# A four-layer graph kernel: one Strassen product moved to another PSUM bank, and seven products for ten pairs of the third layer's first block

## The chip, the cores and the metric

The kernel runs on one core of one Trainium2 chip. The metric is the device time of one execution in microseconds, as a median of several runs. A profile is taken of one execution apart; its span runs from the first to the last instruction that the profiler saw.

Five engines work side by side[...]: TensorE (PE in the profile, its weight loads PEld), VectorE (DVE), ScalarE (ACT), GpSimd (POOL) and the queue of SyncE (SP), which issues DMAs. [...]

## The reference, cut to what matters

Four graph layers in float32 run over 4096 nodes with 256 features and one adjacency matrix of 4096 x 4096. Each is an attention over the neighbours, followed by a residual sum and a layernorm over the 256 features. The change lies in the third layer, and in helpers that it shares with the fourth:

```python
def _L2_gnn_ref(x, adj, W, a):
    h = x @ W
    e = (h @ a[:D, 0])[:, None] + (h @ a[D:, 0])[None, :]
    e = jnp.where(e > 0, e, NEG_SLOPE * e)
    attention = jax.nn.softmax(jnp.where(adj > 0, e, MASK_VAL), axis=1)
    return jax.nn.elu(attention @ h)

x = _layernorm(x + _L0_gnn_ref(...))   # four heads, additive scores
x = _layernorm(x + _L1_gnn_ref(...))   # four heads, query and key
x = _layernorm(x + _L2_gnn_ref(x, adj, L2_gnn_W, L2_gnn_a))
x = _layernorm(x + _L3_gnn_ref(...))   # cosine scores, half of the features kept
```

## The kernel before, in words

The features of all nodes stay in SBUF as `X`: 32 tiles of 128 nodes x 256 features. The nodes that receive are taken in eight blocks `b` of 512; for each block a sum over all 32 tiles of sending nodes is built in PSUM. In layers three and four the sending tiles are taken two at a time: `g` counts these 16 pairs (`NP`). Layer three applies its matrix W only after the sum.

**Weights.** `weights(b, g)` of the third layer (`additive_one`) makes the unnormalised attention weights of one pair in `prob`, two tiles of 128 x 512. It issues the mask's DMA on SP (four buffers), computes `r` on ScalarE into PSUM (L566), and joins `r`, a factor of the sending node and the mask on VectorE (L567).

**Sums, plain and with seven products.** The sum of a pair is a product of (2 x 128 sending nodes) x (2 x 128 features) with (2 x 128 sending nodes) x (2 x 256 receiving nodes): a 2 x 2 by 2 x 2 block product. Done plainly it takes eight block products, here four matmuls of 512 columns (L581). Strassen's form in Winograd's variant takes seven matmuls of 256 columns (`product`, L446) on mixed operands. `mix_features` (L429 to L432) makes four mixed feature blocks for two pairs at a time: `mixed[q]` serves pairs 2q and 2q+1, and is made once and used in all blocks. `mix_weights` (L436 to L438) makes four mixed weight blocks for each pair of each block: L436 is on VectorE, L437 and L438 are on GpSimd in the third layer and on VectorE in the fourth.

Block 0 of the third layer is summed plainly into two of the four banks `acc`, because the mixed features are only made while it runs: at each odd `g`, on VectorE. Blocks 1 to 7, and the fourth layer, use seven products.

The seven products of all pairs add up in seven halves of the four banks. `first_half` (L451 to L455) and `second_half` (L459, L460) turn these sums into the four quarters `c` of the result. Bank 3 holds product 0 alone, in its first half; its second half is unused.

**The order.** In the third layer the order on PE, VectorE and ScalarE is written out by hand; GpSimd and SP are ordered by the scheduler. A loop over `i` handles unit `i`'s weights and unit `i - 3`'s sums (`LAG = 3`), and spreads other work over the steps: `finish` brings the block before to its end, `follow` prepares the fourth layer's factors, and the generator `before` brings the last block of the second layer to its end inside block 0. That work joins two partial row sums (L867), transposes on PE (L880, L888, L895), divides and adds (L903 to L912), takes statistics (L156), a root (L161 to L171, partly on GpSimd), scales rows (L186), and takes a dot product per row (L504), from which ScalarE and VectorE make the factors that weights 14 and 15 need (L511 to L513). The last sum of a block is issued ahead of the weights of its step, so that the banks are emptied early.

The fourth layer (`cosine_attention`) is ordered by the scheduler until its ending. Its scores are matmuls of 512 columns (L1118), its mixes are all on VectorE.

## Time and profile before

| what | value |
| --- | --- |
| time, median of 3 runs | 2798.02 us (2794.73 to 2802.38) |
| the profiled execution's own time | 2795.6 us |
| its span | 2793.8 us |
| PE busy | 2774.1 us (99%) |
| VectorE busy | 2289.0 us (82%) |
| ScalarE busy | 1700.7 us (61%) |
| GpSimd busy | 1052.5 us (38%) |
| granted TensorE clock | 1.00 throughout |

The first layer's sums end at 723 us, the second layer's at about 1714 us, the third layer runs from there to about 2165 us, and the fourth to 2794 us. A row of the timeline has its start and its duration in us, the engine, the line of the kernel, what is written and read, the shape, how many instructions it merges, and in brackets how long the engine was idle before it and what ended that. A matmul of float32 leaves two records. "Busy" counts a wait inside an instruction as work.

### The profile page before, as it was taken

Reading aid. Unit: us, or ns where it says so; the run is one execution under the profiler, and the core shown is the slowest. Engines: PE = TensorE matmul, PEld = TensorE weight load, DVE = VectorE, ACT = ScalarE, POOL = GpSimd, SP = SyncE. Lnnn points to the kernel's source line nnn. Section 1 sums busy time; section 2 is a strip of 40 time slices with the busy share of each in tenths; the row PEclk is TensorE's granted clock in tenths of the full one; section 3 lists DMA queues with packets and bytes.
Section 4 is the critical chain, followed back from the end, with each engine's and each line's share of the span. In section 5 each row is a group of like instructions: output and inputs, shape, how many; then the busy total and the mean of one; then the engine's idle time right before and its main releaser. Section 6 shows DMA issues by size and latency. Waiting matters only on the chain. (4 is left out here: it accounts for less than half of the span.)

```text
span 2793.8 us, 50176 instructions
## 1 busy us (share of the span) xinstructions
PE 2774.1 (99%) x19445; PEld 1427.4 (51%) x19445; DVE 2289.0 (82%) x3040; ACT 1700.7 (61%) x2650; POOL 1052.5 (38%) x986
## 2 busy tenths in 40 slices
PE   9999999999999999999999999999999999999999
PEld 5333333333453333333333333788888777777776
DVE  8899999999677788887888878888887877767676
ACT  7899999999336666666666666465556422222222
POOL 0000100100029878778788793345455000000000
PEclk9999999999999999999999999999999999999999
DMA  7566676665339899998988988567778545445442
GB/s 206 107 142 137 139 144 130 137 143 114 70 97 191 186 178 196 191 188 182 197 182 189 192 181 187 168 198 207 183 207 232 121 76 82 74 71 82 75 72 44
DMA packets 275065, 411.92 MB, mean 147 GB/s; under 512 B 54809, under 2 KB 155657, under 8 KB 273930
## 3 DMA queue, kind: packets, MB, share of 16 engines
q0 software_dynamic: 104176, 182.74, 41.3%
q1 hardware_dynamic: 164280, 218.88, 26.7%
q10 hardware_dynamic: 6370, 7.10, 0.7%
q8 instruction: 152, 2.49, 0.4%
q14 instruction: 87, 0.71, 0.1%
HBM read 335.94 MB, written 39.40 MB: 134 GB/s over the span
## 5 line engine op out<-in xcount | busy, mean ns | idle before, releaser
L834 DVE TENSOR_TENSOR prob<-p,mask 128x1024 f32<-128x1024 f32 x512 | 620.0, 1222 | 166.9 <-ACT p L824 159.9
L824 ACT ACTIVATE p<-p,shift 128x1024 f32<-128x1024 f32 x512 | 557.0, 1090 | 317.8 <-PE p L822 317.1
L312 PE MATMUL acc<-prob,V 128*32 128x512 f32 x6144 | 664.0, 592 | 1.2 <-DVE prob L302 1.2
L299 ACT ACTIVATE prob<-row,dst 128x512 f32<-128x512 f32 x1020 | 635.9, 716 | 0.4
L302 DVE SCALAR_TENSOR_TENSOR prob<-prob,mask 128x2048 f32<-128x2048 f32 x256 | 580.6, 2288 | 25.8 <-ACT prob L299 24.8
L844 POOL TENSOR_TENSOR den<-den,prob 128x1024 f32<-128x1024 f32 x220 | 559.8, 2544 | 92.6 <-DVE prob L834 87.2
L822 PE MATMUL p<-qT,kT 64*64 64x512 f32 x4096 | 531.1, 590 | 2.0 <-DVE prob L834 2.0
L858 PE MATMUL acc<-prob,V 64*64 64x512 f32 x4096 | 529.9, 589 | 0.0
L312 PEld LDWEIGHTS acc<-prob,V 128*32 128x32 f32 x6144 | 197.3, 110 | 453.0 <-issue 432.2
L446 PE MATMUL acc<-mix,mixed 128*128 128x256 f32 x1428 | 388.0, 380 | 2.7 <-DVE quarters L460 1.2
L858 PEld LDWEIGHTS acc<-prob,V 64*64 64x64 f32 x4096 | 157.4, 133 | 282.1 <-issue 280.3
L822 PEld LDWEIGHTS p<-qT,kT 64*64 64x64 f32 x4096 | 154.3, 133 | 278.9 <-issue 256.5
L446 PEld LDWEIGHTS acc<-mix,mixed 128*128 128x128 f32 x1428 | 269.5, 190 | 45.0 <-PE acc L446 3.5
L90 POOL COPY tick<-prob 128x1 f32<-128x1 f32 x35 | 38.0, 1086 | 643.0 <-DVE prob L302 642.1
L1130 DVE TENSOR_TENSOR prob<-prob,mask 128x1024 f32<-128x1024 f32 x128 | 156.2, 1220 | 140.5 <-ACT prob L1122 140.1
L850 POOL DMA_DIRECT2D den<-prob x240 | 232.0, 967 | 61.0 <-DVE prob L834 22.3
L446 PE MATMUL acc<-prob,X 128*128 128x256 f32 x952 | 245.7, 380 | 3.4 <-DVE quarters L452 3.3
L1050 POOL DMA_DIRECT2D mask<-in_adjT x64 | 47.7, 745 | 530.1 <-DVE prob L1130 437.6
L446 PEld LDWEIGHTS acc<-prob,X 128*128 128x128 f32 x952 | 180.1, 190 | 84.1 <-issue 56.7
L567 DVE SCALAR_TENSOR_TENSOR prob<-r,own,mask 128x512 f32<-128x512 f32 x252 | 177.1, 744 | 51.3 <-POOL s L169 13.7
L1122 ACT ACTIVATE prob<-p 128x512 f32<-128x512 f32 x144 | 86.1, 598 | 204.1 <-PE p L1118 202.6
L1122 ACT ACTIVATE prob<-g 128x512 f32<-128x512 f32 x112 | 67.0, 598 | 208.7 <-PE g L1118 208.7
(233 smaller groups left out, 2823.1 us busy)
## 6 DMA issues: line engine op xcount, KB each, us to landing
mask<-in_adjT SPq DMA_DIRECT2D x254, 512.0 KB
den<-prob POOLq DMA_DIRECT2D x240, 512.0 KB, 5.3
mask<-edges SPq DMA_DIRECT2D x512, 64.0 KB
mask<-in_adjT POOLq DMA_DIRECT2D x64, 512.0 KB, 5.7
edges<-in_adj POOLq DMA_DIRECT2D x32, 512.0 KB, 9.6
far<-squares SPq DMA_DIRECT2D x16, 512.0 KB
den<-prob SPq DMA_DIRECT2D x16, 512.0 KB
row<-far SPq DMA_DIRECT2D x7, 1024.0 KB
```

The source lines that it names most:

```text
L299: nc.scalar.activation(z[:, h, :], r, AF.Relu, bias=-1.0, scale=dst[:, j, h:h + 1])
L302: nc.vector.scalar_tensor_tensor(z, z, 1.0, mask[m][:, j % MJ, :].unsqueeze(1).to_broadcast([P, H, QW]), OP.add, OP.mult)
L312: nc.tensor.matmul(acc[b][h * G:(h + 1) * G, n, :], part, prob[b, j][:, h, :], start=(j == 0), stop=(j == NT - 1))
L446: nc.tensor.matmul(acc[at][:, half * HW:(half + 1) * HW], w, a, start=(g == 0 and half == 0), stop=(g == NP - 1), skip_group_check=True)
L567: nc.vector.scalar_tensor_tensor(z[:, n, :], r, ga.own[:, j:j + 1], mask[:, n, :], OP.add, OP.mult)
L822: nc.tensor.matmul(p[c * d:(c + 1) * d, r, :], kT[half, c, at:at + d], qT[half, c, cols], start=True, stop=True)
L824: nc.scalar.activation(p, p, AF.Exp, bias=shift)
L834: nc.vector.tensor_tensor(z, p, mask[m][:, j % MJ, :].unsqueeze(1).to_broadcast([P, KC, QW]), OP.mult)
L844: nc.gpsimd.tensor_tensor(to, to, flat, OP.add)
L850: nc.gpsimd.dma_start(to, flat, accum_op=OP.add)
L858: nc.tensor.matmul(acc[b][c][r * d:(r + 1) * d, :], V[half, j, r * d:(r + 1) * d], prob[b, j][half, r, :], start=(j == 0), stop=(j == NH - 1))
L1130: nc.vector.tensor_tensor(z, z, co.mask[b, 2 * g // MJ][:, lo:lo + 2, :], OP.mult)
```

## The change

It has four parts.

- Product 1 (`n` = 1) adds up in the second half of bank 3 instead of the first half of bank 0. `first_half` copies both halves of bank 3 on ScalarE, its first sum on VectorE covers 256 columns instead of 512, and a further VectorE operation at the end adds product 0 to quarter 0. This holds for all blocks of the third and fourth layer.
- Block 0 of the third layer uses seven products for pairs 4 to 13 (`apart`). The other six pairs are summed by `plain`: eight matmuls of 256 columns into four bank halves, among them the first half of bank 0 that product 1 has left. That half is copied (`more`) and added to quarter 2.
- The mixed features are made earlier and on other engines: a table `mixing` says at which step. Tiles 2, 0 and 1 stay on VectorE (steps 1, 4 and 14); of tiles 3, 4, 5, 6 and 7 three of the four operations go to GpSimd and L431 stays on VectorE (steps 2, 2, 3, 4 and 16).
- The second layer's end takes its root on VectorE instead of GpSimd, one factor on ScalarE instead of VectorE, and its steps are spread a little differently.

In the changed program GpSimd's order, after the last operation of the second layer (L850 before, L862 now), is: L429 of tiles 3 and 4, L430 of 3 and 4, L432 of 3 and 4, the same for tiles 5 and 6, and then L437 and L438 of pair 4 and so on. VectorE's order starts with weights 0, the four operations of tile 2, weights 1, L431 of tiles 3 and 4, weights 2, L431 of tile 5, weights 3, the four operations of tile 0, L431 of tile 6, a dot product, weights 4. Later lines move by 10 to 15 in number: L566 and L567 become L579 and L580, L581 becomes L453 (`plain`), L451 to L460 become L459 to L470.

```diff
@@ -423,41 +423,51 @@
     NP = NT // 2
     HW = QW // 2
 
-    def mix_features(t, q):
+    def mix_features(t, q, eng=nc.vector):
 
         x = X[:, 4 * q:4 * q + 4, :D].rearrange("p (g n) (h f) -> p g n h f", n=2, h=2)
-        nc.vector.tensor_tensor(t[:, :, 0, :], x[:, :, 0, 1, :], x[:, :, 0, 0, :], OP.subtract)
-        nc.vector.tensor_tensor(t[:, :, 1, :], x[:, :, 1, 1, :], t[:, :, 0, :], OP.add)
+        eng.tensor_tensor(t[:, :, 0, :], x[:, :, 0, 1, :], x[:, :, 0, 0, :], OP.subtract)
+        eng.tensor_tensor(t[:, :, 1, :], x[:, :, 1, 1, :], t[:, :, 0, :], OP.add)
         nc.vector.scalar_tensor_tensor(t[:, :, 2, :], x[:, :, 1, 1, :], -1.0, x[:, :, 0, 1, :], OP.mult, OP.subtract)
-        nc.vector.tensor_tensor(t[:, :, 3, :], x[:, :, 1, 0, :], t[:, :, 1, :], OP.subtract)
+        eng.tensor_tensor(t[:, :, 3, :], x[:, :, 1, 0, :], t[:, :, 1, :], OP.subtract)
 
     def mix_weights(s, z, eng):
 
         nc.vector.tensor_tensor(s[:, :2, :], z[:, 0, :].rearrange("p (h i) -> p h i", h=2), z[:, :, HW:], OP.subtract)
         eng.tensor_tensor(s[:, 2, :], z[:, 0, :HW], s[:, 1, :], OP.subtract)
-        eng.tensor_tensor(s[:, 3, :], z[:, 1, :HW], s[:, 2, :], OP.subtract)
+        return eng.tensor_tensor(s[:, 3, :], z[:, 1, :HW], s[:, 2, :], OP.subtract)
 
     def product(acc, z, s, t, g, n):
 
         even, odd = X[:, 2 * g, :D], X[:, 2 * g + 1, :D]
-        at, half, w, a = ((3, 0, even[:, :P], z[:, 0, :HW]), (0, 0, odd[:, :P], z[:, 1, :HW]),
+        at, half, w, a = ((3, 0, even[:, :P], z[:, 0, :HW]), (3, 1, odd[:, :P], z[:, 1, :HW]),
                           (0, 1, t[:, 1], s[:, 2]), (1, 0, t[:, 0], s[:, 1]), (1, 1, odd[:, P:], s[:, 3]),
                           (2, 0, t[:, 2], s[:, 0]), (2, 1, t[:, 3], z[:, 1, HW:]))[n]
-        nc.tensor.matmul(acc[at][:, half * HW:(half + 1) * HW], w, a, start=(g == 0 and half == 0),
+        nc.tensor.matmul(acc[at][:, half * HW:(half + 1) * HW], w, a, start=(g == 0 and n in (0, 2, 3, 5)),
                          stop=(g == NP - 1), skip_group_check=True)
 
+    def plain(acc, z, g):
+
+        for at, to, f, lo in ((3, 1, 0, 0), (0, 0, 1, HW), (1, 1, 1, 0), (2, 1, 0, HW)):
+            for n in range(2):
+                nc.tensor.matmul(acc[at][:, to * HW:(to + 1) * HW], X[:, 2 * g + n, f * P:(f + 1) * P],
+                                 z[:, n, lo:lo + HW], start=(g == 0 and n == 0), stop=(g == NP - 1),
+                                 skip_group_check=True)
+
     def first_half(c, one, acc):
 
         nc.scalar.copy(one, acc[3][:, :HW])
-        nc.vector.tensor_tensor(c[:, :2, :], one.unsqueeze(1).to_broadcast([P, 2, HW]),
-                                acc[0].rearrange("p (h i) -> p h i", h=2), OP.add)
+        nc.scalar.copy(c[:, 0, :], acc[3][:, HW:])
+        nc.vector.tensor_tensor(c[:, 1, :], one, acc[0][:, HW:], OP.add)
         nc.vector.tensor_tensor(c[:, 2, :], c[:, 1, :], acc[1][:, :HW], OP.add)
         nc.vector.tensor_tensor(c[:, 3, :], c[:, 2, :], acc[1][:, HW:], OP.add)
 
-    def second_half(c, acc):
+    def second_half(c, acc, one=None):
 
         nc.vector.tensor_tensor(c[:, 1:3, :], c[:, 1:3, :], acc[2][:, :HW].unsqueeze(1).to_broadcast([P, 2, HW]), OP.add)
         nc.vector.tensor_tensor(c[:, 1, :], c[:, 1, :], acc[2][:, HW:], OP.add)
+        if one is not None:
+            nc.vector.tensor_tensor(c[:, 0, :], c[:, 0, :], one, OP.add)
 
     def quarters(c, k):
 
@@ -504,13 +514,13 @@
                 nc.vector.tensor_tensor_reduce(junk, X[:, t, :D], self.a_row[:, n, :], 1.0, 0.0, OP.mult, OP.add,
                                                self.dot[:, t, n:n + 1])
 
-        def factors(self, b):
+        def factors(self, b, times=nc.vector.tensor_scalar_mul):
 
             t = slice(b * QB, (b + 1) * QB)
             d = self.dot[:, t, 1]
             nc.scalar.activation(self.dst[:, t], d, AF.Exp)
             nc.scalar.activation(self.own[:, t], d, AF.Exp, scale=self.slope)
-            nc.vector.tensor_scalar_mul(self.less[:, t], self.own[:, t], -1.0)
+            times(self.less[:, t], self.own[:, t], -1.0)
 
         def sources(self, b):
             src = fin.tile([P, QB], FP, name="src2")
@@ -542,6 +552,9 @@
             ps = pool(lay, "gb_ps", 2, space=PSUM)
             edges = adjT.rearrange("(t p) i -> p t i", p=P)
             mixed, acc, prob, mix, mvs, roots, kept, drawn, ys, far_y = {}, {}, {}, {}, {}, {}, {}, {}, {}, {}
+            apart = range(4, 14)
+            mixing = {1: ((2, nc.vector),), 2: ((3, nc.gpsimd), (4, nc.gpsimd)), 3: ((5, nc.gpsimd),),
+                      4: ((0, nc.vector), (6, nc.gpsimd)), 14: ((1, nc.vector),), 16: ((7, nc.gpsimd),)}
 
             def bank():
                 return ps.tile([P, QW], FP, name="g")
@@ -565,30 +578,28 @@
                     r = pr.tile([P, QW], FP, name="r")
                     nc.scalar.activation(r, ga.row_of(b), AF.Relu, bias=ga.less[:, j:j + 1], scale=ga.dst[:, j:j + 1])
                     nc.vector.scalar_tensor_tensor(z[:, n, :], r, ga.own[:, j:j + 1], mask[:, n, :], OP.add, OP.mult)
-                if b:
+                if b or g in apart:
                     s = mix[b, g] = zp.tile([P, 4, HW], FP, name="mix")
-                    mix_weights(s, z, nc.gpsimd)
+                    return mix_weights(s, z, nc.gpsimd)
 
             def sums(b, g):
                 if g == 0:
                     acc[b] = [pa.tile([P, QW], FP, name=f"acc{n}") for n in range(4)]
-                if b:
+                if (b, g) in mix:
                     for n in range(7):
                         product(acc[b], prob[b, g], mix[b, g], mixed[g // 2][:, g % 2], g, n)
                 else:
-                    for j in range(2 * g, 2 * g + 2):
-                        for c in range(KC):
-                            nc.tensor.matmul(acc[b][c], X[:, j, c * P:(c + 1) * P], prob[b, g][:, j % 2, :],
-                                             start=(j == 0), stop=(j == NT - 1))
+                    plain(acc[b], prob[b, g], g)
                 if g == NP - 1:
                     c = kept[b] = op.tile([P, 4, HW], FP, name="quarters")
-                    if b:
-                        first_half(c, op.tile([P, HW], FP, name="one"), acc[b])
-                        second_half(c, acc[b])
-                    else:
-                        nc.scalar.copy(c[:, :2, :], acc[b][0].rearrange("p (h i) -> p h i", h=2))
-                        nc.vector.tensor_copy(c[:, 3, :], acc[b][1][:, :HW])
-                        nc.vector.tensor_copy(c[:, 2, :], acc[b][1][:, HW:])
+                    if b == 0:
+                        more = fin1.tile([P, QW], FP, name=f"kept{KC}")[:, :HW]
+                        nc.scalar.copy(more, acc[b][0][:, :HW])
+                    one = op.tile([P, HW], FP, name="one")
+                    first_half(c, one, acc[b])
+                    second_half(c, acc[b], one)
+                    if b == 0:
+                        nc.vector.tensor_tensor(c[:, 2, :], c[:, 2, :], more, OP.add)
 
             def project(bank, b, k):
                 po = drawn[b, k] = bank()
@@ -645,29 +656,30 @@
             LAG = 3
             units = [(b, g) for b in range(NB) for g in range(NP)]
             fixed = {mybir.EngineType.PE, mybir.EngineType.DVE, mybir.EngineType.Activation}
-            before = tail(bank)
+            before, last = tail(bank), None
             with tc.manual_schedule(engines=fixed):
                 for i in range(len(units) + LAG):
                     b, g = units[i - LAG] if i >= LAG else (-1, 0)
                     if g == NP - 1:
                         sums(b, g)
+                    for q, eng in mixing.get(i, ()):
+                        t = mixed[q] = keep.tile([P, 2, 4, P], FP, name=f"mixed{q}")
+                        with tc.issue_after(getattr(last, "ins", last)) if i >= NP else nullcontext():
+                            mix_features(t, q, eng)
                     if i < len(units):
-                        weights(*units[i])
+                        last = weights(*units[i]) or last
                     if b >= 0:
                         if g < NP - 1:
                             sums(b, g)
                         if b:
                             finish(b - 1, g)
                         else:
-                            for _ in range({4: 3, 6: 2, 7: 3, 8: 4, 9: 3, 10: 4}.get(g, 0)):
+                            for _ in range({4: 3, 6: 2, 7: 3, 8: 5, 9: 3, 10: 3}.get(g, 0)):
                                 next(before, None)
                             if g == 11:
                                 follow.start()
                             elif g == 14:
                                 follow.centre(bank())
-                            if g % 2:
-                                t = mixed[g // 2] = keep.tile([P, 2, 4, P], FP, name=f"mixed{g // 2}")
-                                mix_features(t, g // 2)
                         if b > 2 and g == 0:
                             follow.prepare(bank, b - 3, 1)
                         if b > 1 and g in (2, 4, 6, 8, 9, 10, 11, 12, 13, 14, 15):
@@ -1000,14 +1012,14 @@
                 yield
             v, r, n = begin_root(mv)
             yield
-            end_root(v, r, n, nc.gpsimd)
-            lift_mean(mv, v, r, nc.gpsimd)
+            end_root(v, r, n)
+            lift_mean(mv, v, r)
             yield
             for k in range(QB):
                 scale_row(X[:, b * QB + k, :D], mv, r, k)
                 ga.dots(b * QB + k, (1,))
                 yield
-            ga.factors(b)
+            ga.factors(b, nc.scalar.mul)
             rows_done()
             yield
         return tail
@@ -1183,7 +1195,9 @@
 
             def outputs(b):
                 c = cp.tile([P, 4, HW], FP, name="quarters")
-                first_half(c, cp.tile([P, HW], FP, name="one"), acc[b])
+                one = cp.tile([P, HW], FP, name="one")
+                first_half(c, one, acc[b])
+                nc.vector.tensor_tensor(c[:, 0, :], c[:, 0, :], one, OP.add)
                 squares_far(b, 0, (c[:, 0, :], c[:, 3, :]))
                 second_half(c, acc[b])
                 squares_far(b, 1, (c[:, 1, :], c[:, 2, :]))
@@ -1231,8 +1245,9 @@
 
                 for k in range(2):
                     direct(k)
-                first_half(c, cp.tile([P, HW], FP, name="one"), acc[b])
-                second_half(c, acc[b])
+                one = cp.tile([P, HW], FP, name="one")
+                first_half(c, one, acc[b])
+                second_half(c, acc[b], one)
                 for k in range(2):
                     others(k)
                     twice_sum(k)
```

## The prediction

> **What bounds the kernel now.** The page's first part comes first, then busy time by stretch, TensorE's waits, and the timeline of the third layer's first block. TensorE is busy almost throughout; that share is not its peak, so the stretches and pitches matter.

> ```profile
> PE 2774.1 (99%) x19445; PEld 1427.4 (51%) x19445; DVE 2289.0 (82%) x3040; ACT 1700.7 (61%) x2650; POOL 1052.5 (38%) x986
> ```

> By stretch (length, busy time of PE, PEld, DVE, ACT, POOL, each with its count): the first row is the third layer's block 0, the second most of its block 1, the last the fourth layer.

> ```profile
> 1713.80:1772.00 58.20, 58.17 (x164) 26.53 (x161) 46.90 (x102) 28.39 (x45) 3.72 (x10) 1.00 0.68 190
> 1772.00:1826.00 54.00, 52.93 (x245) 46.21 (x244) 48.23 (x90) 30.54 (x50) 26.77 (x40) 1.00 0.60 164
> 2165.00:2778.00 613.00, 612.54 (x2326) 440.60 (x2325) 437.01 (x830) 177.88 (x348) 46.78 (x64) 1.00 0.48 79
> ```

> Block 0 keeps PE full, VectorE at 81% and GpSimd nearly idle. Two pitches follow from the PE timeline (56 records in a row) and the chain (98 in a row):

> ```profile
> 1743.69 24.20 PE L581 MATMUL acc<-prob,X 128*128 128x512 f32 x56
> 2144.16 21.15 PE acc L446 x98
> ```

> A 512-column record takes 0.431 us, a 256-column one 0.2155 us; an f32 matmul leaves two. A pair costs 8 x 0.431 = 3.45 us plain and 14 x 0.2155 = 3.02 us with seven products. PE's waits in the two last layers (total, times, longest):

> ```profile
> PE acc L446 <- DVE quarters L452: 3.3, 4, 1.0
> PE acc L446 <- DVE quarters L460: 1.2, 6, 0.2
> PE acc L446 <- DVE quarters L591: 1.1, 1, 1.1
> ```

> They lie where one block's banks are emptied for the next. Counting each start that is later than the pitch, the timeline gives 1.3 us at the change from block 0 to 1, 0.55 to 1.9 us at each of the next six, and 0.1 us at most changes of the fourth layer; 12.1 us in all.

> VectorE runs little ahead in block 0 (start, duration, idle before, releaser):

> ```profile
> 1715.72 1.45 DVE L567 SCALAR_TENSOR_TENSOR prob<-r,own,first_mask 128x512 f32<-128x512 f32 x2 [1.67 <-ACT r L566]
> 1724.62 1.41 DVE L567 SCALAR_TENSOR_TENSOR prob<-r,own,mask 128x512 f32<-128x512 f32 x2 [3.90 <-DMA mask<-in_adjT]
> 1754.58 0.41 DVE L186 TENSOR_SCALAR X<-X,mv,r 128x256 f32<-128x256 f32 x1 [2.25 <-POOL mv L191]
> 1762.02 1.46 DVE L567 SCALAR_TENSOR_TENSOR prob<-r,own,mask 128x512 f32<-128x512 f32 x2 [0.85 <-ACT r L566]
> 1769.00 0.83 DVE L430 TENSOR_TENSOR mixed<-X,mixed 128x256 f32<-128x256 f32 x1
> ```

> The fourth row is pair 14's weights, finished at 1763.5; PE takes them at 1764.4. So VectorE becomes the limit once PE gains about 1 us. The last row, 0.83 us instead of 0.42, meets a GpSimd operation.

> [...] The trace agrees (0.42 to 0.83 us; L567, whose r is in PSUM, stays at 0.74). It also shows who wins when GpSimd's operations follow without a gap:

> ```profile
> 1891.01 0.74 POOL L438 TENSOR_TENSOR mix<-prob,mix 128x256 f32<-128x256 f32 x1
> 1891.70 0.73 POOL L437 TENSOR_TENSOR mix<-prob,mix 128x256 f32<-128x256 f32 x1
> 1890.99 1.73 DVE L504 CUSTOM_DVE_ANT_0 h<-X,a_row 128x256 f32<-128x256 f32 x1
> ```

> The VectorE operation sat through both. This recurs at 1948.05 and 2061.93; at 2005.33 VectorE got in after one: three of four. [...]

> **The change part by part.** All against the profiled execution, 2795.6 us (span 2793.8 and 1.8 around it); the median shown, 2798.0, is 2.4 above it.

> 1. Seven products for pairs 4 to 13: 10 x (3.45 - 3.02) = -4.3 us of PE. The six plain pairs become 16 records of 0.2155: the same 3.45; their doubled weight loads (0.19 each) hide under the matmuls as L446's do now.

> 2. Block changes. n=1 moves from bank 0 to bank 3, so VectorE is first needed by n=2, 0.43 us into the block instead of 0.22, and its first sum shrinks from 512 to 256 columns. At 1938 VectorE, not PE, sets the pace: L452 starts at 1937.98 when its queue lets it. The five sums then run 0.45, 0.45, 0.53, 0.72, 0.42 apart where the first step was 0.75, so bank 2 is free at 1940.55 instead of 1940.85, and PE's n=5 starts about 0.35 us sooner. Six such changes: -2.1 us. The second ScalarE copy of bank 3 (0.35 us, L451's time) must precede n=0: at 1936.98 + 0.35 it costs n=0 some 0.15 us, absorbed by the later wait for bank 2. The closing add (0.34) trades with the 0.27 saved: +0.07 us of VectorE a block, under its 19% idle. The change to block 1 should lose its stall, since bank 3 is final 2.6 us and bank 0 1.7 us before the block's end: -1.3 us. Fourth layer: 0.1 us stalls, nothing. At the end the add is done near 2780.9, and PE's L1208 needs it at 2781.7: nothing.

> 3. VectorE in block 0. Before: five mixes ahead of pair 14's weights, 7.3 us. After: three mixes (4.4), four single L431 (1.4), ten L436 (6.1), the roots moved from GpSimd (six dependent small operations, some 0.9 by their 0.16 each in the fourth layer), less L513 (0.17): +5.3 us of work. The waits of 1.67 and 3.90 take the mixes moved forward (5.5 us of them), and the 2.25 us root wait goes. Summing the queue from 1712.65: 45.7 us of work, 1.9 left of the mask wait and some 0.5 on PE and ScalarE put pair 14's weights at 1760. The unhindered PE wants them at 1764.4 - 4.3 = 1760.1: a tie.

> 4. [...] GpSimd gets twelve mix operations (pairs of tiles interleaved, so no operation waits for the one just before) behind its last DMA issue, which ends at 1714.76, then two per pair. [...] In that time VectorE's order has two of mix 2's four operations, three L431 and mix 0, all with two SBUF inputs, in front of weights 1 to 4. PE wants weights 1 at 1717.3. At best each waits one operation (+0.4 us); at worst the third operation of mix 2 sits until 1723.1. I take the three-in-four odds, about three GpSimd operations for each: weights 1 near 1719, weights 2 near 1725, weights 4 done near 1731 instead of 1726.0. PE loses some 4 us there. Adding later collisions (dots, joins, L436: +2.7 us by 0.34 each), pair 14's weights come at 1760 + 5 + 2.7, near 1767.5. Queued behind are weights 15, block 1's first pairs and the first L461, but PE spends 7.8 us on pairs 14, 15 and the centring, so VectorE recovers. PE enters pair 14 on its first half, at 1767.0, and block 0 ends at 1774.8, against 1772.0 + 1.3 of stall before: +1.5 us.

> 5. ScalarE's extra small copy (L513's work, 0.2) and GpSimd's mix 7 (2.1 us, needed 15 pairs later) are hidden.

> Sum: +1.5 - 2.1 = -0.6, rounded with the chance that VectorE wins oftener to **-2 us**: 2793.6 for a profiled execution, 2796.0 as median.

> **The rivals.**
> *PE-bound:* [...] all PE terms arrive: -4.3 - 1.3 - 2.1 = -7.7, 2790.3. For it: VectorE's 5.6 us of early waits. Against: the 1.73 us row.
> *Half-way:* each VectorE operation waits once. Weights 14 at 1762.7, block end 1769.8: -3.5 - 2.1 = -5.6, 2792.4.
> *Slower, by one mechanism:* GpSimd never lets VectorE in between 1714.8 and 1723.1. Weights 1 come at 1725.0, PE's pair 1 starts 7.1 us late, and later collisions cost twice my 2.7. Weights 14 near 1771.5, block end 1778.8: +5.5 - 2.1 = +3.4, 2801.4. It decides once PE enters pair 14 later than 1768.0. Three odds in four per operation, over twelve, speak against a full shut-out.
> *Not what it says:* the bank change gives nothing because ScalarE's second copy takes the place of VectorE's wait: 2.1 us less gain, 2798.

> **How the numbers follow.** 0.3% is 8.4 us, about what a measurement of this kernel can tell from no change. Likeliest case 0.45, half-way 0.2, PE-bound 0.12, slower 0.15, no bank gain 0.08. All centres lie within 8.4 us, so a verdict outside needs a wrong size as well; the three runs shown spread over 7.7 us. PE-bound half passes the bound, half-way a third, the rest little: faster 0.2; slower 0.14; same 0.66. Range 2789 to 2802 from PE-bound to slower; the likeliest case alone, 2793 to 2799.

> **What would show it.** Right: pair 14 entered late, a PE wait on L580 near 1717 to 1725, L429 to L431 at 1 to 3 us in that stretch, no wait for L463 entering block 1, n=5 waiting 0.1 to 0.2 us less. Wrong: those operations at 0.42 us (PE-bound), or PE in pair 14 after 1768. Masks landing later, or new stalls in the fourth layer, would break it another way.

## The result, and the profile after

The changed kernel takes 2799.8 us (median of 22 runs, 2795.8 to 2805.2) against 2796.1 us for the kernel before (22 runs, 2794.3 to 2802.4). The ratio is 1.0013, with a 95% interval of 1.0007 to 1.0019: about 3.7 us slower, where 2 us faster was forecast. The profiled execution took 2805.0 us (span 2803.2), so it is one of the longer ones. Of this, 4.4 us are two waits outside block 0 that the profile before doesn't have in this size: 1.6 us for ScalarE at 2146 us, and 2.75 us at 2591 us, where VectorE stood waiting for a far transfer. Nothing here shows that they come from the change.

The busy shares hardly move. First the page's line, then the stretches by busy time (length, then PE, PEld, DVE, ACT, POOL with their counts, the granted clock, the share of DMA and GB/s): block 0 of the third layer, its block 1, and the fourth layer.

```profile
PE 2773.1 (99%) x19553; PEld 1451.2 (52%) x19553; DVE 2301.7 (82%) x3060; ACT 1703.4 (61%) x2668; POOL 1077.2 (38%) x1015
```
```profile
1713.50:1783.35 69.85, 59.16 (x272) 49.35 (x269) 64.09 (x111) 29.28 (x49) 31.12 (x41) 0.90 0.62 166
1783.35:1835.20 51.85, 51.85 (x242) 45.62 (x241) 45.95 (x86) 29.44 (x50) 25.42 (x38) 1.00 0.56 164
2168.00:2789.00 621.00, 618.22 (x2353) 445.53 (x2352) 441.34 (x844) 184.87 (x368) 48.74 (x67) 1.00 0.48 80
```

Block 0 took 58.2 us and now takes 69.85, with TensorE idle for 10.7 of them and a granted clock of 0.90. Block 1 runs without a gap. From one first product to the next, blocks 1 to 6 are together 5.4 us shorter than before. But for the two stray waits the loss lies in block 0, and TensorE's waits name the place (total, times, longest):

```profile
PE acc L453 <- DVE prob L580: 10.1, 2, 7.5
PE acc L446 <- POOL mix L437: 0.6, 1, 0.6
PE acc L446 <- DVE quarters L468: 0.6, 3, 0.2
PE acc L446 <- DVE quarters L463: 0.4, 2, 0.2
```

The waits for the emptied banks (the tiles `acc`, 128 x 512 float32 each), 4.5 us before on L452 and L460, are 1.0 us on L463 and L468 and 0.4 on ScalarE's copy. In their place stand two waits for VectorE's weights (L580): one of 7.5 us ahead of pair 1, one of 2.5 us ahead of pair 14. The timeline of VectorE, then of GpSimd, at the first of them (start, duration, line):

```profile
1713.67 9.25 DVE L429 TENSOR_TENSOR mixed<-X 128x256 f32<-128x256 f32 x1
```
```profile
1714.00 1.89 POOL L429 TENSOR_TENSOR mixed<-X 128x256 f32<-128x256 f32 x2
1715.38 1.85 POOL L430 TENSOR_TENSOR mixed<-X,mixed 128x256 f32<-128x256 f32 x2
...
1720.83 1.79 POOL L432 TENSOR_TENSOR mixed<-X,mixed 128x256 f32<-128x256 f32 x2
```

One VectorE operation that takes 0.41 us by itself (shown below) lasts 9.25 us: until 0.3 us after GpSimd's run of twelve is over. VectorE's next rows come in the order of the program, L430 at 1722.95 and weights 1 at 1723.97. So here the two engines met inside an operation that had already started. TensorE's rows after the two waits, and its granted clock by stretches of 3.41 us, follow:

```profile
1724.76 10.46 PE L453 MATMUL acc<-prob,X 128*128 128x256 f32 x36 [7.53 <-DVE prob L580]
1773.75 5.45 PE L453 MATMUL acc<-prob,X 128*128 128x256 f32 x16 [2.52 <-DVE prob L580]
```
```profile
1716.05:1719.46 3.41, 1.18 (x6) 0.70 (x4) 3.41 (x1) 0.04 (x1) 3.41 (x6) 1.00 1.06 246
1719.46:1722.88 3.42, 0.00 (x0) 0.00 (x0) 3.42 (x1) 0.00 (x0) 3.16 (x5) 0.50 1.03 273
1722.88:1726.29 3.41, 1.53 (x4) 1.20 (x5) 3.38 (x9) 1.48 (x2) 0.00 (x0) 0.50 0.22 82
1726.29:1729.70 3.41, 3.41 (x10) 2.65 (x9) 3.38 (x7) 2.80 (x4) 0.00 (x0) 0.50 0.36 114
1729.70:1733.12 3.42, 3.42 (x18) 3.00 (x17) 3.39 (x10) 1.44 (x3) 0.00 (x0) 1.00 0.64 193
```

That was not foreseen: with each wait TensorE's clock is halved for whole stretches of 3.41 us (three from 1719.46, one from 1774.08), and 256-column records come every 0.427 us instead of 0.2155. Counting every start that is later than the pitch, block 0 loses 16.1 us (0.5 before): 7.5 and 2.5 in the two waits, 2.6 and 1.6 in the slow clock after each, 0.6 for a mixed weight, and small gaps after each wait. By the pitches TensorE's own work is 4.3 us less, as forecast: 58.2 - 0.5 - 4.3 + 16.1 = 69.5, against 69.85, so that some 4.0 of the 4.3 us arrived.

### The profile page after: what moved, and what is told of

Same layout as the page of the kernel before. It is cut to its first block, busy times and chain, and to the rows that moved or that the text cites. A ratio compares the mean times of both kernels' runs of the same rounds, so it can differ in the third digit from the quotient of the medians.

```text
span 2803.2 us, 50488 instructions
## 1 busy us (share of the span) xinstructions
PE 2773.1 (99%) x19553; PEld 1451.2 (52%) x19553; DVE 2301.7 (82%) x3060; ACT 1703.4 (61%) x2668; POOL 1077.2 (38%) x1015
## 5 line engine op out<-in xcount | busy, mean ns | idle before, releaser
L446 PE MATMUL acc<-mix,mixed 128*128 128x256 f32 x1488 | 404.1, 380 | 4.5 <-DVE mix L437 2.7
L446 PEld LDWEIGHTS acc<-mix,mixed 128*128 128x128 f32 x1488 | 281.2, 190 | 47.9 <-DVE mix L437 3.6
L862 POOL DMA_DIRECT2D den<-prob x240 | 231.3, 964 | 62.6 <-DMA den<-prob 23.2
L446 PE MATMUL acc<-prob,X 128*128 128x256 f32 x992 | 254.8, 379 | 0.4 <-ACT quarters L460 0.4
L446 PEld LDWEIGHTS acc<-prob,X 128*128 128x128 f32 x992 | 188.2, 190 | 79.7 <-issue 58.0
L580 DVE SCALAR_TENSOR_TENSOR prob<-r,own,mask 128x512 f32<-128x512 f32 x252 | 176.9, 743 | 49.3 <-ACT r L579 14.8
```

The source lines that it names most:

```text
L446: nc.tensor.matmul(acc[at][:, half * HW:(half + 1) * HW], w, a, start=(g == 0 and n in (0, 2, 3, 5)), stop=(g == NP - 1), skip_group_check ...
L580: nc.vector.scalar_tensor_tensor(z[:, n, :], r, ga.own[:, j:j + 1], mask[:, n, :], OP.add, OP.mult)
L862: nc.gpsimd.dma_start(to, flat, accum_op=OP.add)
```

## The experiments

Two causes were set against each other first: GpSimd's unbroken run that keeps VectorE out, and VectorE's added work alone.

**All mixes on VectorE.**

```
-            mixing = {1: ((2, nc.vector),), 2: ((3, nc.gpsimd), (4, nc.gpsimd)), 3: ((5, nc.gpsimd),), ...
+            mixing = {1: ((2, nc.vector),), 2: ((3, nc.vector), (4, nc.vector)), 3: ((5, nc.vector),), ...
```

> The changed kernel with every mix of block 0 on VectorE; GpSimd keeps only the third and fourth mixed weights. Theory (GpSimd's twelve operations in one unbroken run keep VectorE out, and TensorE's clock halves after the long wait): no VectorE operation between 1713 and 1725 us takes over 1 us, no TensorE wait over 2 us there, granted clock 1.0 through block 0, block 0 lasts 56 to 59 us instead of 69.85, and the kernel takes 2788 to 2792 us, 8 to 11 below the changed kernel. Rival (VectorE simply has too much work ahead of pairs 1 to 4, on whichever engine the mixes stand): the wait moves to pair 3 or 4 and is again 5 us or more, block 0 stays above 65 us, and the kernel at 2797 to 2800.

Measured: 2794.2 us, ratio 0.9994 (0.9986 to 1.0002). The operation at 1713 takes 0.41 us:

```profile
1712.98 0.41 DVE L429 TENSOR_TENSOR mixed<-X 128x256 f32<-128x256 f32 x1
```

The 7.5 us wait is gone, so GpSimd's mixes were its cause. The rest fell between the two theories: block 0 takes 61.4 us, neither 56 to 59 nor above 65. VectorE is busy 95% of 1713 to 1783, and TensorE waits 0.9 us for a mixed weight, 0.7 for the attention's sum, and 1.9 for its reciprocals:

```profile
PE g L907 <- DVE rden L915: 1.9, 1, 1.9
PE acc L446 <- POOL mix L437: 0.9, 1, 0.9
PE g L892 <- DVE den L879: 0.7, 1, 0.7
```

So even without GpSimd's mixes, seven products for these ten pairs, with the mixes in this order, make block 0 3.2 us longer than before. They don't pay here: the bank part alone, measured below on the same chip, is 2.7 us faster.

**GpSimd's mixes in a chain.** Each tile's mix waits for the last operation of the one before, so the operations no longer stand ready all at once.

```
-                        with tc.issue_after(getattr(last, "ins", last)) if i >= NP else nullcontext():
-                            mix_features(t, q, eng)
+                        after = last if i >= NP else chain if eng is nc.gpsimd else None
+                        with tc.issue_after(getattr(after, "ins", after)) if after is not None else nullcontext():
+                            mixes = mix_features(t, q, eng)
+                        if eng is nc.gpsimd:
+                            chain = mixes
...
```

> The changed kernel with one addition: each of GpSimd's mixes waits for the last operation of the one before, and within a mix each operation already waits for the one before or is free to follow it, so that the twelve operations no longer stand ready all at once. Theory (the run keeps VectorE out because GpSimd's next operation is always ready): VectorE gets in where an operation waits for its forerunner, its operations last at most about 1.5 us each, weights 1 are ready at about 1719 to 1721 us, TensorE's wait is 2 to 4 us instead of 7.5, and the kernel takes 2792 to 2797 us. Rival [...]: the operation of VectorE that begins at 1713.7 still lasts 8 us or more, the wait stays above 6 us, and the kernel at 2799 to 2801.

Measured: 2795.8 us, ratio 1.0003 (0.9995 to 1.0011). VectorE's timeline:

```profile
1713.97 1.83 DVE L429 TENSOR_TENSOR mixed<-X 128x256 f32<-128x256 f32 x1
1715.83 0.83 DVE L430 TENSOR_TENSOR mixed<-X,mixed 128x256 f32<-128x256 f32 x1
1716.59 0.95 DVE L431 SCALAR_TENSOR_TENSOR mixed<-X 128x256 f32<-128x256 f32 x1
1717.45 0.94 DVE L432 TENSOR_TENSOR mixed<-X,mixed 128x256 f32<-128x256 f32 x1
```

The same twelve operations, and VectorE gets in after each. TensorE's wait ahead of pair 1 falls from 7.5 to 1.6 us. GpSimd is busy for 3.25 of the 3.41 us from 1716.75, all of them in the changed kernel. What matters in this stretch is not that GpSimd works, but whether its next operation is ready when the last one ends: no hold passes 1.83 us here, against 9.25. Block 0 still takes 63.4 us: the wait at pair 14 stays at 2.5 us (the second and longest of the two in this row), though the early one is nearly gone.

```profile
PE acc L453 <- DVE prob L580: 4.1, 2, 2.5
```

**A run of six.** Tiles 3 and 4 alone on GpSimd, the rest on VectorE.

> The changed kernel with two tiles' mixes (3 and 4) on GpSimd and the other six on VectorE: GpSimd's run of ready operations is six long instead of twelve. Theory (a VectorE operation with two SBUF inputs that meets the run waits for its end): the operation caught at 1713.7 lasts as long as six GpSimd operations at 0.68 to 0.7 us, 4.2 to 5 us instead of 9.25, weights 1 come near 1720.5, TensorE waits 3 to 4 us. Rival (one unlucky grab, of a length that has nothing to do with the run): the caught operation lasts 9 us again, or under 2.

Measured in a single profiled run (2799.9 us, too little to compare times): the caught operation lasts 5.20 us, and the wait 3.5.

```profile
1712.97 5.20 DVE L429 TENSOR_TENSOR mixed<-X 128x256 f32<-128x256 f32 x1
```

Six operations less shorten it by 9.25 - 5.20 = 4.05 us, 0.675 each, which is GpSimd's time from start to start (0.68). In both runs the operation ends 0.3 us after the last of GpSimd's. In these two runs the hold is as long as GpSimd's run.

**The bank part alone.** The kernel before with the second product in bank 3's second half and the order of sums that goes with it.

```
-        at, half, w, a = ((3, 0, even[:, :P], z[:, 0, :HW]), (0, 0, odd[:, :P], z[:, 1, :HW]),
+        at, half, w, a = ((3, 0, even[:, :P], z[:, 0, :HW]), (3, 1, odd[:, :P], z[:, 1, :HW]),
```

> The kernel before with one part of the change: Strassen's second product in the second half of the fourth bank, and the order of additions that goes with it; block 0 and all mixes as before. Theory (the seven block changes in the third layer gain 5.4 us, as the lengths of blocks 1 to 6 in the changed kernel say): blocks 1 to 6 as in the changed kernel, block 0 58.2 us, kernel about 2790.7 us, ratio about 0.998. Rival A (the prediction's size: six changes at 0.35 us, 2.1 us in all): 2794. Rival B (part of the gain in block 1 belongs to the end of block 0, not to the banks): block 1 keeps 53.1 us and the sum is 4.1.

Measured: 2791.6 us, ratio 0.9985 (0.9978 to 0.9991), 4.4 us below before. Late starts at the six changes from block 1 to 7 sum to 8.3 us before and 4.7 here. The change into block 1 keeps its stall (1.3 us both times), since block 0 ends as before here. Blocks 1 to 6 are together 2.8 us shorter, not the theory's 5.4, and block 1 keeps its 53.1 us: rival B holds. In the changed kernel this stall is gone, but the new order of block 0's plain products is not enough for that. The kernel with all mixes on VectorE has the same order and 1.2 us of stall. VectorE's first sum at this change, in the changed kernel and then with all mixes on VectorE:

```profile
1782.51 0.42 DVE L461 TENSOR_TENSOR quarters<-one,acc 128x256 f32<-128x256 f32 x1 [1.23 <-ACT one L459]
```
```profile
1774.68 0.40 DVE L461 TENSOR_TENSOR quarters<-one,acc 128x256 f32<-128x256 f32 x1
```

In the first, VectorE waits for ScalarE's copy of the bank and starts 0.85 us ahead of block 1's first product (1783.36). In the second it comes from other work and starts 0.5 us after it (1774.21). Run again on another chip:

> The bank part alone once more, beside the other two on their chip, since the kernel before stood 3 us apart in the two calls so far. Theory: ratio 0.9985 as in the first call, and the same waits. Rival (the 0.15% was that chip's scatter): ratio within 0.0005 of 1.

Measured: 2793.0 us, ratio 0.9988 (0.9981 to 0.9994); late starts at the six changes 3.7 us, blocks 1 to 6 3.9 us shorter. The bank part alone beats both kernels. Block 0, which it leaves as it was, took 58.2 us in the first trace and 59.1 in this one, so a difference of 1 us in block 0 between two single traces says nothing.

**What halves the clock.** Twelve dead additions on VectorE ahead of weights 1, in the kernel before; GpSimd idle. In this cut `<a_row>` stands for a long view of the tile `a_row`.

```
+                    if i == 1:
...
+                        for _ in range(12):
+                            nc.vector.tensor_tensor(mixed[0][:, 0], <a_row>, <a_row>, OP.add)
...
```

> The kernel before with dead work added: twelve VectorE additions of 128x512, about 0.6 to 0.7 us each, ahead of weights 1; GpSimd does nothing there. TensorE so waits about 6 us after pair 0, with no engine shut out. Theory (a wait of TensorE of that length is by itself what halves its clock, for some 5 to 10 us): granted clock 0.5 from about 3.4 us after the wait began, matmuls of 128x512 at 0.85 us instead of 0.43 for 3 to 6 us after it, and the kernel 8 to 12 us above before. Rival (the half clock belongs to what the changed kernel does, GpSimd and VectorE together or seven products a pair): the clock stays at 1.0 after the wait, and the kernel is 5 to 8 us above before, the wait and no more.

Measured: 2804.7 us, ratio 1.0034 (1.0020 to 1.0047), 8.7 us above before. A 5.8 us wait, and the clock is halved from 1720.13 to 1726.96:

```profile
1716.72:1720.13 3.41, 0.00 (x0) 0.00 (x0) 3.25 (x5) 0.00 (x0) 0.00 (x0) 1.00 1.06 249
1720.13:1723.54 3.41, 1.03 (x2) 0.52 (x3) 3.15 (x6) 1.05 (x2) 0.00 (x0) 0.50 0.83 255
1723.54:1726.96 3.42, 3.42 (x6) 1.35 (x5) 3.27 (x7) 3.18 (x5) 0.00 (x0) 0.50 0.31 66
1726.96:1730.37 3.41, 3.41 (x9) 1.51 (x8) 3.38 (x9) 1.70 (x3) 0.00 (x0) 1.00 0.81 264
```

A wait of 5.8 us is enough here, without GpSimd and without seven products. Here the kernel does pay: block 0 takes 66.5 us, 8.3 more, 5.8 for the wait and about 2.3 for the clock.

**The wait filled with dead work on TensorE.** The first attempt was mis-sized: sixteen f32 matmuls left 32 records and took 13.9 us, not 6.9.

```
+                        if i == LAG:
+                            idle = bank()
+                            for _ in range(16):
+                                nc.tensor.matmul(idle, X[:, 0, :P], prob[0, 0][:, 0, :], start=True, stop=True)
```

> The changed kernel with dead work added on TensorE: sixteen matmuls of 128x512 into a bank that nobody reads, between pair 0 and pair 1, 16 x 0.43 = 6.9 us, in the place of the 7.5 us wait. VectorE and GpSimd are untouched, weights 1 come at 1724.8 as before. Theory (the wait itself halves the clock): granted clock 1.0 from 1713 to 1770, 0.2155 us a record after the wait instead of 0.427, and pairs 1 to 13 run 2.4 us earlier; if the later collisions with GpSimd don't take it back, the kernel falls to 2797 to 2798. Rival A (the halving comes from the load, more engines at once): the clock falls to 0.5 all the same, 2799 to 2801. Rival B (the 2.4 us are slack, because VectorE's weights 14 set the end of block 0): clock 1.0 but the wait at pair 14 grows from 2.5 to about 5 us, 2799.8.

Measured: 2806.1 us, ratio 1.0028 (1.0016 to 1.0039). The clock stays at 1.0 through the stretch (1717.50 to 1740.00) although VectorE is held for 9.24 us just as long, so in this stretch the load did not halve it. The total says nothing, since the dead work outlasted the wait by 6 us. One row is telling: counted from the end of VectorE's hold, TensorE comes to pair 14 about 3.5 us later than in the changed kernel (51.8 us after it, not 48.3), and still waits 2.5 us:

```profile
PE acc L453 <- DVE prob L580: 2.5, 1, 2.5
```

Then with eight:

> The changed kernel with eight dead matmuls of 128x512 between pair 0 and pair 1 (each leaves two records of 0.43 us: 6.9 us in all), so that the dead work fits into the 7.5 us wait and lengthens nothing. Theory (the wait itself halves the clock, and the first half-clock stretch costs 2.5 us): the wait ahead of pair 1 shrinks to about 0.6 us, granted clock 1.0 from 1713 until the wait at pair 14, which stays at about 2.5 us because it hangs on TensorE's own pace; block 0 at 67 to 67.5 us against 69.85, ratio about 1.0004. Rival (the clock's halving costs the kernel nothing, since VectorE sets the end of block 0): block 0 at 69.5 to 70 us, the wait at pair 14 at 5 us, ratio 1.0013.

Measured: 2802.0 us, ratio 1.0013 (1.0007 to 1.0019), the same as the changed kernel. The clock is 1.0 until 1770.9, and the wait ahead of pair 1 is 0.7 us; but block 0 takes 69.3 us. The 2.5 us came back as new waits: 0.9 us for the reciprocals, and three of 0.8 to 1.0 near the end, with a half-clock stretch at 1770.87:

```profile
1768.33 1.36 PE L446 MATMUL acc<-prob,X 128*128 128x256 f32 x4 [0.99 <-DVE prob L580]
1770.62 1.87 PE L446 MATMUL acc<-mix,mixed 128*128 128x256 f32 x4 [0.93 <-POOL mix L437]
1775.57 3.95 PE L453 MATMUL acc<-prob,X 128*128 128x256 f32 x16 [0.83 <-DVE prob L580]
```

The theory fell (its 1.0004 lies outside the interval). The rival holds in the total and in block 0, though it had put the wait at pair 14, at 5 us, where 0.8 was measured: in the changed kernel the first half-clock stretch costs nothing that the total shows. VectorE, held back 8.8 us, hands the time back as waits before block 0 ends.

**The wait at pair 14.** Tile 7's mix, which GpSimd did at 1769.6 to 1772.1, given to it eight pairs later (16 becomes 24 in the table of mixes):

> The changed kernel with the mix of tile 7 given to GpSimd eight pairs later, in block 1. Theory (its three operations at 1769.6 to 1772.1 hold up the chain to pair 14's weights): the wait at 1773.7 falls from 2.5 us to 1.2 or less, the clock keeps 1.0 at 1774 (1.7 us more), and the kernel takes 2796 to 2797. Rival (the collisions with the third and fourth mixed weights and the roots moved to VectorE make pair 14 late): wait 2 us or more, 2799 to 2800.

Measured: 2800.0 us, ratio 1.0002 (0.9994 to 1.0010; its chip had before at 2799.5). The wait falls to 1.3 us, just above the theory's 1.2, the clock stays at 1.0 there, and block 0 takes 67.6 us, 2.3 less. By the ratios it is 3 us against the changed kernel, with intervals that just overlap. So about half of the wait at pair 14 is tile 7's. Then pairs 8 to 13 made plain again:

```
-            apart = range(4, 14)
+            apart = range(4, 8)
```

> The changed kernel with seven products for pairs 4 to 7 alone; pairs 8 to 13 plain again. All else, GpSimd's run of twelve too, as in the changed kernel. Theory (a second limit lies in block 0: the chain on VectorE from the reciprocals of the attention's last rows to pair 14's weights takes over 20 us, and the six plain pairs that TensorE works in that time last 6 x 3.45 = 20.7; seven products take 2.6 us off that cover and put 0.6 us a pair on VectorE): the 7.5 us wait and its half clock stay, but the wait at pair 14 falls from 2.5 us to under 0.5 and the clock keeps 1.0 near 1774, so that block 0 comes out shorter, at 67 to 68 us against 69.85, although TensorE has 2.6 us more to do; kernel 1 to 2 us below the changed kernel, ratio about 1.0007. Rival (seven products gain 0.43 us a pair wherever they stand, and the wait at pair 14 comes from the early delay): block 0 at 71 to 72.5 us, ratio 1.002.

Measured: 2799.6 us, ratio 1.0008 (0.9999 to 1.0016), an interval that also holds the changed kernel's 1.0013. What tells is the trace: the wait at pair 14 is gone, and block 0 takes 67.1 us although TensorE has 2.6 us more to do. TensorE's row runs from pair 8 to 14 without a gap:

```profile
1750.67 24.34 PE L453 MATMUL acc<-prob,X 128*128 128x256 f32 x112
```

**Two tries at a better version**, both on the bank part, with mixes on VectorE and roots on GpSimd. Seven products for pairs 8 to 13:

> The bank part of the change, and seven products for pairs 8 to 13 alone, with all mixes on VectorE: those of tiles 4, 5, 6 and 0 in the two early waits for ScalarE and the mask, the other four after pair 14's weights; the roots stay on GpSimd as before. Theory (block 0 can take seven products as far as VectorE has room for them and no GpSimd run stands beside it): TensorE's work falls by 6 x 0.43 = 2.6 us, VectorE's grows by 6 x 0.61 = 3.7 us, of which 5 us of filled waits pay; waits in block 0 under 1 us in all, block 0 at 56 us, kernel 2788.5 to 2789.5. Rival (VectorE sets the pace of block 0 as soon as any pair gets seven products): pair 14 waits 2 us or more, block 0 at 58 us or above, 2791 to 2793.

Measured: 2798.6 us, ratio 0.9997 (0.9988 to 1.0005), block 0 at 60.1 us. The rival was right:

```profile
1764.02 5.68 PE L453 MATMUL acc<-prob,X 128*128 128x256 f32 x16 [1.89 <-DVE prob L580]
```

The 2.6 us gained in pairs 8 to 13 come back as a 1.9 us wait and a half-clock stretch (1765.29 to 1768.71), and block 1, into which two of the mixes were put, is 2.5 us longer. Seven products for pairs 4 to 7:

> The bank part of the change, and seven products for pairs 4 to 7, ahead of the chain to pair 14's weights; all mixes on VectorE, four of them in its waits (for ScalarE, for the mask, for GpSimd's roots), none between the reciprocals and pair 14's weights but the one in the wait for the roots; roots on GpSimd as before. Theory (same second limit): no TensorE wait over 0.5 us and clock 1.0 through block 0, block 0 at 58.2 - 4 x 0.43 = 56.5 us, kernel 1.7 us below the bank part alone. Rival (VectorE is late from pair 4 on, its queue full): waits of 1 us or more at the attention's last products or at pair 14, block 0 at 58 us or more, kernel equal to or above the bank part alone.

Measured: 2794.5 us, ratio 0.9991 (0.9985 to 0.9998), against 0.9988 for the bank part on the same chip. No wait at pair 14 and a full clock, as the theory had it; but VectorE is late at the attention's last sum and, by 0.4 us, at the reciprocals:

```profile
PE g L896 <- DVE den L883: 1.9, 1, 1.9
```

That is the rival's case, and the 1.7 us are gone: block 0 takes 59.1 us, as for the bank part on this chip.

## Why the prediction was wrong

**The step that failed is part 4, how GpSimd's run meets VectorE.** "I take the three-in-four odds, about three GpSimd operations for each": these odds were read from runs of two operations in the trace before, and carried over to a run of twelve as if each boundary were a new draw. Three runs show it otherwise: the hold lasted as long as GpSimd's next operation stood ready (9.25 us for twelve, 5.20 for six), and was broken after each operation that waited for its forerunner (0.83 to 1.83 us). It also took the first operation of tile 2's mix, not the third. The prediction's own three cases fit this: VectorE got in where GpSimd's next operation, L438 (at 1892.51, 1949.56 and 2063.46), needed the result of the L437 just before it. The fourth, at 2005.33, does not fit: VectorE got in although the next operation stood ready. So the odds were counted over boundaries of two kinds. The slower rival, "GpSimd never lets VectorE in", was the true case: it had the twelve operations, at 0.69 us each, end at 1723.1 (they did at 1722.6), and put weights 1 at 1725.0, and TensorE started at 1724.8. The prediction's own sign of being wrong, TensorE in pair 14 after 1768, came too: 1773.75. The rival was given a chance of 0.15, because "Three odds in four per operation, over twelve, speak against a full shut-out"; the boundaries were not independent draws. That its +3.4 us lies so near the measured 3.7 is luck: it had block 0 6.8 us longer and the six changes 2.1 us shorter, where the traces have 11.6 us and some 4. Taking GpSimd's mixes away is worth about 5 us by the ratios (1.0013 to 0.9994). VectorE's record starts 0.33 us before GpSimd's first mix, and yet it is VectorE that waits, through the whole run. A DMA issue of GpSimd's was under way at that moment (1713.41, 1.05 us); with all mixes on VectorE the same issue (until 1713.76) stands beside the operation of 0.41 us, so by itself it held nothing there.

**Part 3, the tie at pair 14, failed too, and would have failed without the long hold.** It summed VectorE's queue from 1712.65 as if the work could flow (its terms add up to 1760.75, not 1760). But part of it starts at TensorE's own products after pair 8: the reciprocals, the normalisation, the roots, the dots, weights 14. In the kernel before that chain runs from 1742.80 to the first half of weights 14 at 1762.77, 19.97 us, and TensorE's record of pair 14 starts at 1764.30, 21.5 us after the chain's start: 1.5 us to spare. Seven products take 2.6 us off the 21.5. In the changed kernel L436, the roots and the collisions lengthen the chain to 22.5 (1751.16 to 1773.7). Its start before, then its start and end in the changed kernel:

```profile
1742.80 0.28 DVE L903 RECIPROCAL rden<-g 128x8 f32<-128x8 f32 x2 [0.52 <-PE g L888]
```
```profile
1751.16 0.28 DVE L915 RECIPROCAL rden<-g 128x8 f32<-128x8 f32 x2
...
1772.96 1.40 DVE L580 SCALAR_TENSOR_TENSOR prob<-r,own,mask 128x512 f32<-128x512 f32 x2
```

That makes a wait: 22.5 - 18.9 - 0.8 of other gaps on the way = 2.8, measured 2.5. It doesn't hang on the early hold: the chained run has the same 2.5 us after an early wait of 1.6, and the run with pairs 8 to 13 alone has 1.9 us with no mixed features on GpSimd. With pairs 8 to 13 plain it is gone in spite of the full hold. With all mixes on VectorE it is 0.3 us, where TensorE had already lost 1.9 us at the reciprocals.

**Part 1 was about right in size and wrong in worth:** the products cost some 4 us less, but VectorE, which has to mix for them, and the chain above bound block 0.

**Part 2 had the mechanism and missed the size.** Six changes were put at 0.35 us each, 2.1 us; the bank part alone gave 4.4 and 3.4 us, and late starts at these changes fall by 3.6 to 4.6 us. (The second run's interval, 0.9981 to 0.9994, reaches down to 1.7 us and so holds the 2.1; the late starts do not.) The 0.35 was worked out at one change, at 1938, and given to all six. In the two traces the late starts there go from 1.7 us to 1.9 and 0.4, and at the change before it, at 1881, from 0.9 us to none in both, so one change does not stand for six. In the changed kernel the product that opens bank 3 waited once for ScalarE's second copy (L460): 0.41 us, at 2113.92. The stall into block 1 was lost as foretold (1.3 us), though only where VectorE has nothing else to do ahead of the sums, and the fourth layer gained nothing, as foretold. Without this gain the changed kernel would, by these sums, be some 8 us slower than before.

**Not in the prediction:** TensorE's clock. Half-clock stretches followed waits of 1.9 to 7.5 us (in one run two of 0.99 and 0.93 us close together), though not the 2.75 us at 2591 nor the 1.9 us of the last try, and whether they cost anything depended on what was late next: 2.3 us in the kernel with dead additions, nothing measurable after the first wait here. That the second stretch (1.6 us after pair 14) costs its full length was not tried by itself.

**Open:** where the stray waits come from that make 4.4 of the 5.2 us by which the profiled run stands above its median; how block 0 of the changed kernel spreads between executions, of which only one was traced; and why VectorE got in at 2005.33.

## What to carry to other kernels

Here twelve ready GpSimd operations held a VectorE operation with two SBUF operands (L429) for 9.25 us and six held it for 5.20, while in a chain no hold passed 1.83 us. Where a trace shows such holds, price them at the length of the whole run, or make each operation wait for the one before it, as the chained kernel does. An engine's work can't be summed as one queue where part of it starts at another engine's product; find the anchor, and compare the chain with the cover that is left after the saving. Before adding up what a faster TensorE saves, ask whether the engine that feeds it has the time.

## What the runs showed of the hardware

| kernel | stretch from | TensorE idle in it | clock in the next |
| --- | --- | --- | --- |
| dead additions | 1716.72 | 100% | 0.5 |
| changed | 1770.66 | 74% | 0.5 |
| six on GpSimd | 1717.58 | 72% | 0.5 |
| changed | 1716.05 | 65% | 0.5 |
| all mixes on VectorE | 1742.79 | 56% | 0.5 |
| bank part, pairs 8 to 13 | 1761.88 | 56% | 0.5 |
| changed | 2589.86 | 49% | 1.0 |
| changed | 2146.13 | 47% | 1.0 |
| mixes in a chain | 1716.75 | 46% | 1.0 |
| changed | 736.43 | 37% | 1.0 |
| changed | 2593.28 | 31% | 1.0 |

So a 1.9 us wait halved the clock in the kernel with all mixes on VectorE (first two rows), and a wait of 2.75 us, split over two stretches at 2591 us of the changed kernel, did not (last two rows):

```profile
1742.79:1746.20 3.41, 1.49 (x12) 1.25 (x11) 3.31 (x7) 1.48 (x2) 2.44 (x4) 1.00 0.22 74
1746.20:1749.62 3.42, 3.42 (x9) 2.66 (x8) 3.35 (x6) 0.00 (x0) 0.46 (x1) 0.50 0.77 237
```
```profile
2589.86:2593.28 3.42, 1.73 (x7) 0.80 (x5) 0.01 (x1) 0.60 (x1) 0.00 (x0) 1.00 0.56 113
2593.28:2596.69 3.41, 2.35 (x9) 1.72 (x10) 3.38 (x11) 0.32 (x1) 0.00 (x0) 1.00 0.02 2
```

At 0.5, stretches idle for 100% and 55% (1719.46 and 1722.88 in the changed kernel) and for 70% (1720.13 with the dead additions) were followed by another at 0.5; fully busy ones (1726.29 and 1774.08, and 1723.54) by one at 1.0.

**VectorE beside GpSimd's mixes.** In the changed kernel L514 took 0.83 us instead of 0.42 at 1768.20, and L186 0.81 instead of 0.41 at 1768.96; in the chained kernel two of L431 took 1.30 us instead of 0.75 at 1719.64. L580, whose `r` is in PSUM, kept its 1.40 us for two (chained kernel, 1718.32), and L156 its 0.40 (changed kernel, 1757.40).
